# SyncE fetches some rows of the second layer one by one, in place of two GpSimd gathers in one pair of chunks in 20

## The chip, the cores and the metric

The kernel runs on one core of a Trainium2 chip. A core has TensorE (PE in the profile; its weight loads are PEld), VectorE (DVE), ScalarE (ACT), GpSimd (POOL) and SyncE (SP). SyncE does no arithmetic on tensors; it issues transfers and can work with registers. The metric is the device time of one execution in microseconds, and the median of several runs is quoted.

## The reference

A graph network with two layers over 12,500 nodes and 200,000 edges. The edges are sorted by their destination.

```python
h = relu(layernorm(x))
x = x + gcn(h)            # out-degree norm, sum over the edges, in-degree norm, 32x32 matrix
h = relu(layernorm(x))
x = x + edge_mlp(h)       # this is the second layer

def edge_mlp(x):          # for each edge from j to i
    msg = concat(x[i], x[j] - x[i])
    h = relu(msg @ W1 + b1)      # 64 to 64
    h = relu(h @ W2 + b2)        # 64 to 128
    h = relu(h @ W3 + b3)        # 128 to 64
    m = h @ W4 + b4              # 64 to 32
    return segment_sum(m, i) / max(count(i), 1)
```

The first product is linear in x[i] and x[j], so it is taken once per node: the kernel keeps two tables in DRAM, `tab_i` and `tab_j`, each with one row of 64 floats per node, and the first hidden layer of an edge is relu(tab_i[i] + tab_j[j]).

## The kernel before

The edges stand in tiles of 128; four tiles make a chunk (512 edges), and two chunks make a pair. There are 391 chunks and so 196 pairs (`NPAIR`). The first layer ends with `update_nodes`, which writes `tab_j` and `tab_i` (L513, L514). The second layer is one loop over pairs, written as a software pipeline with its order fixed by hand:

```python
for m in range(NPAIR + last):
    if m < NPAIR:
        gather_in(m)
    if m + AHEAD + 1 < NPAIR:
        prepare(m + AHEAD + 1)
    advance(running)
    for lag, stage in ((last, fourth), (4, third), (3, second), (1, first)):
```

- `gather_in(m)` lets GpSimd gather the rows of `tab_j` for the eight tiles of pair m, one indirect transfer per tile (L211). Each takes 128 row numbers from `src_j` and brings 128 rows of 256 bytes into the tile `gj`. There are six `gj` buffers.
- `prepare(m)` lets SyncE load what a pair needs besides: `ai`, the window of `tab_i` rows that its sorted destinations fall into (L858, five buffers), and `row`, the destinations relative to that window, repeated on 128 partitions (L861, four buffers). `AHEAD` is 2, so in step m of the loop SyncE issues these for pair m + 3.
- `turn(m)` compares `row` with the partition's number on VectorE (L868), which gives a one-hot matrix `turned`.
- `first(m)` is TensorE's first stage: a small matmul on `gj` (L884), four transposes of `gj` (L888), and the product of `ai` with `turned` added to them (L892). ScalarE applies the relu. `second`, `third` and `fourth` follow three, four and five steps of the loop later: the two further layers (L906, L916), with their evictions on ScalarE (L908) and VectorE (L919), and the sum over destinations (L934).

SyncE executes its instructions in the order of the program: a pair's `ai` and `row` stand behind whatever was issued on SyncE ahead of them. The framework gives SyncE's and ScalarE's transfers eight completion semaphores in turn, so a transfer waits for the one that used its semaphore before.

At L970 every engine loads one number from a tile into a register, and SyncE checks its range there. It is the only register load of the kernel.

Of the kernel before, what the change touches and what calls it, by code (L numbers as in the profile page):

```python
# [8 lines left out]
F32 = mybir.dt.float32  # L9
BF16 = mybir.dt.bfloat16  # L10
F16 = mybir.dt.float16
I32 = mybir.dt.int32
# [4 lines left out]
P = 128  # L17
N_NODES = 12500
N_EDGES = 200000
D = 32  # L20
HID = 64
# [4 lines left out]
OFF = 48  # L26
# [7 lines left out]
TPC = 4  # L34
CHUNK = TPC * P
NCH = -(-N_EDGES // CHUNK)
NTR = -(-N_EDGES // P)
# [39 lines left out]
DPAD = (DIR + NDG * GD) * CHUNK  # L77

PC = 32

NROW = NPAD + P

# [2 lines left out]
def gnn_kernel(  # L85
# [20 lines left out]
    nc = tc.nc  # L106
# [14 lines left out]
    tab_j = dram.tile([NPAD, HID], F32, name="tab_j")  # L121
# [9 lines left out]
    def parts(rows):  # L131

        return rows.rearrange("(p j) c -> p j c", p=NPART)
# [23 lines left out]
    xp = fp.tile([NPART, P, D], F32, name="xp")  # L157
    pieces = [slice(j, j + PC) for j in range(0, P, PC)]
    for at in pieces:
# [5 lines left out]
    o = dst.offset + DIR * CHUNK  # L165
# [3 lines left out]
    ident = const.tile([P, P], F32, name="ident")  # L169
# [40 lines left out]
    def gather(tile_ap, table, col):  # L210
        nc.gpsimd.indirect_dma_start(  # L211
            out=tile_ap, out_offset=None, in_=table,
            in_offset=bass.IndirectOffsetOnAxis(ap=col, axis=0))
# [10 lines left out]
    o = 1 + D  # L224
# [15 lines left out]
    for at in pieces:  # L240
        h, a = hx[:, at, :D], xp[:, at, :]
        m = fp.tile([NPART, PC], F32, name="la_m", bufs=2)
        nc.vector.tensor_reduce(m, a, AX.X, OP.add)
        nc.vector.tensor_scalar(m, m, 1.0 / D, None, op0=OP.mult)
        nc.vector.tensor_sub(h, a, m[:, :, None].to_broadcast([NPART, PC, D]))
        nc.vector.tensor_mul(a, h, h)
        v = fp.tile([NPART, PC], F32, name="la_v", bufs=2)
        nc.vector.tensor_reduce(v, a, AX.X, OP.add)
        nc.vector.tensor_scalar(v, v, 1.0 / D, EPS, op0=OP.mult, op1=OP.add)
        sd = fp.tile([NPART, PC], F32, name="la_sd", bufs=2)  # L250
        nc.scalar.activation(sd, v, AF.Sqrt)
        nc.vector.reciprocal(v, sd)
        nc.vector.scalar_tensor_tensor(
            h, h, 0.0, v[:, :, None].to_broadcast([NPART, PC, D]), op0=OP.max, op1=OP.mult)
        nc.sync.dma_start(parts(tab_h[OFF:, :])[:, at, :], hx[:, at, :])
    first.close()
    src_j = stay.tile([P, NT], I32, name="src_j")

    def gather_chunk(rows, table, g):
        for t in range(min(TPC, NTR - g * TPC)):  # L260
            c = g * TPC + t
            gather(rows[:, t, :], table, src_j[:, c : c + 1])
# [23 lines left out]
    with tc.tile_pool(name="deg", bufs=3) as hp, tc.tile_pool(  # L286
        name="deg_ps", bufs=1, space=bass.MemoryType.PSUM
# [42 lines left out]
        for b in batches:  # L330
            to = min(EARLY, RAW + -(-(EARLY - RAW) * (b // (HG * HT) + AHEAD_HG) // len(batches)))
            if to > gathered:
                c = slice(gathered * TPC, to * TPC)
# [6 lines left out]
            for t in range(b, min(NTR, b + HG * HT)):  # L340
                g, i = divmod(t - b, HT)
# [12 lines left out]
        for at in pieces:  # L354
# [4 lines left out]
            for k in range(3):  # L359
                t = terms[:, :, k * D : (k + 1) * D]  # L360
# [19 lines left out]
        for b in range(0, NT, P):  # L380
            n = min(P, NT - b)
# [51 lines left out]
    with tc.tile_pool(name="flag", bufs=1) as fp, tc.tile_pool(  # L433
        name="flag_ps", bufs=1, space=bass.MemoryType.PSUM
# [131 lines left out]
    def advance(running):  # L566

        for r in list(running):
            if next(r, running) is running:
                running.remove(r)  # L570
# [12 lines left out]
    def halves(m):  # L583
        return [k for k in range(2) if 2 * m + k < NCH]
# [4 lines left out]
    with tc.tile_pool(name="e0", bufs=8) as sp, tc.tile_pool(name="nu", bufs=1) as np_, tc.tile_pool(  # L589
        name="direct", bufs=1) as dp, tc.tile_pool(name="e0_ps", bufs=1, space=bass.MemoryType.PSUM) as pp, tc.tile_pool(  # L590
        name="nu_ps", bufs=1, space=bass.MemoryType.PSUM) as np_ps:
# [194 lines left out]
        for m in range(EARLY, DIR + LAG + 1):  # L786
# [6 lines left out]
            i = m - EARLY  # L793
# [11 lines left out]
            later, r = divmod(i, LATER)  # L805
# [13 lines left out]
    with tc.manual_schedule(), tc.tile_pool(name="prep", bufs=3) as prep, tc.tile_pool(name="e1", bufs=3) as ep, tc.tile_pool(name="fn", bufs=2) as fp, tc.tile_pool(  # L819
        name="p1_ps", bufs=2, space=bass.MemoryType.PSUM  # L820
# [32 lines left out]
        def prepare(m):  # L853

            v = live[m] = {"turned": []}
            n, g = len(halves(m)), 2 * m
            ai = v["ai"] = prep.tile([P, 2, HID], F32, name="ai", bufs=5)
            nc.sync.dma_start(ai[:, :n], bass.AP(  # L858
                tensor=tab_i.tensor, offset=tab_i.offset + STEP * g * HID, ap=[[HID, P], [STEP * HID, n], [1, HID]]))
            row = v["row"] = prep.tile([P, 2, CHUNK], F16, name="row", bufs=4)  # L860
            nc.sync.dma_start(row[:, :n], bass.AP(  # L861
                tensor=rel_row.tensor, offset=rel_row.offset + g * CHUNK, ap=[[0, P], [CHUNK, n], [1, CHUNK]]))

        def turn(m):
            v = live[m]
            for k in halves(m):
                turned = prep.tile([P, CHUNK], F32, name=f"turned{k}", bufs=3)
                nc.vector.tensor_tensor(  # L868
                    turned, v["row"][:, k], part_f.to_broadcast([P, CHUNK]), op=OP.is_equal)
                v["turned"].append(turned)  # L870

        def gather_in(m):
            gj = live[m]["gj"] = ep.tile([P, TPC, 2, HID], F32, name="gj", bufs=6)
            if len(halves(m)) < 2 or (2 * m + 2) * TPC > NTR:
                nc.vector.memset(gj, 0.0)
            for k in halves(m):
                g = 2 * m + k
                gather_chunk(gj[:, :, k, :], tab_j[:, :], g)

        def first(m):  # L880
            v = live[m]
            p1 = pp1.tile([P, TPC, P], F32, name="p1")

            nc.tensor.matmul(  # L884
                p1[:1, 0, : 2 * TPC], ident[:, :1], v["gj"][:, :, :, 0].rearrange("p t k -> p (t k)"), start=True, stop=True,
                skip_group_check=True)
            for t in range(TPC):
                nc.tensor.matmul(  # L888
                    p1[:, t, :], v["gj"][:, t].rearrange("p k c -> p (k c)"), ident, is_transpose=True,
                    start=(t == 0), stop=False, skip_group_check=True)  # L890
            for k in halves(m):
                nc.tensor.matmul(  # L892
                    p1[k * HID : (k + 1) * HID].rearrange("p t e -> p (t e)"), v["ai"][:, k], v["turned"][k],
                    start=False, stop=True, skip_group_check=True)
            h1 = ep.tile([P, CHUNK], F32, name="h1", bufs=4)
            nc.scalar.activation(h1, p1.rearrange("p t e -> p (t e)"), AF.Relu)  # L896
            v["h1"] = h1
# [40 lines left out]
        def add_messages(k4):  # L938
            q, i = divmod(k4, J)
            ps = group_ps.pop(k4)  # L940
            for k in range(2):
                chunks = len(range(k4 * GRP + k, min(NCH, (k4 + 1) * GRP), 2))
                if chunks:
                    s = slice(k * HID, (k + 1) * HID)
                    sums.add(s, P * k4 + STEP * k, ps[s, : 2 * STEP * (chunks - 1) + W])
            if i == J - 1 or k4 == NGRP - 1:
                running.append(finish_nodes(q))
# [4 lines left out]
        last = 5  # L952
        for m in range(NPAIR + last):
            if m < NPAIR:
                gather_in(m)
            if m + AHEAD + 1 < NPAIR:
                prepare(m + AHEAD + 1)
            advance(running)
            for lag, stage in ((last, fourth), (4, third), (3, second), (1, first)):
                if 0 <= m - lag < NPAIR:  # L960
                    stage(m - lag)
                if stage is fourth and m >= lag and ((m - lag) % (GRP // 2) == GRP // 2 - 1 or m - lag == NPAIR - 1):
                    add_messages((m - lag) // (GRP // 2))
            if m + 1 < NPAIR:
                turn(m + 1)
# [5 lines left out]
    with tc.If(bad > 0):  # L971
        sums0 = dram.tile([NROW, D + 1], F32, name="sums0")
        sums1 = dram.tile([NROW, D], F32, name="sums1")
        with tc.tile_pool(name="gp", bufs=1) as gp, tc.tile_pool(name="ge", bufs=1) as ge, tc.tile_pool(
            name="ge_ps", bufs=1, space=bass.MemoryType.PSUM
# [49 lines left out]
            with tc.For_i(0, NTR, 1) as i:  # L1025
                s, d, same, r = edges(i)
# [13 lines left out]
            for q in range(NQ):  # L1040
                n = min(J, NBLK - J * q)
# [10 lines left out]
            with tc.For_i(0, NTR, 1) as i:  # L1052
                s, d, same, r = edges(i)
                gi = ge.tile([P, HID], F32, name="g_gi")
                gather(gi, tab_i[:, :], d)
                gj = ge.tile([P, HID], F32, name="g_gj")
# [27 lines left out]
            c = gp.tile([P, NBLK], F32, name="g_c")  # L1084
# [39 lines left out]
```

## Time and profile before

| | us |
|---|---|
| median of 3 runs | 3516.55 (3509.39 to 3517.01) |
| profiled execution, its own time | 3509.95 |
| its span in the profile | 3508.2 |
| first gather of the second layer | 1525.7 |
| last gather of the second layer ends | 3480.0 |

The span is what the profile covers; the execution's own time is 1.75 us more. The second layer takes from 1525.7 us to the end, some 1980 us for 196 pairs. In the profile's lists a group of instructions is a line of the kernel, an engine, an operation and the tiles by name; then come the count, the busy time with the mean of one in ns, and the idle time of that engine just before these instructions with what ended most of it. "issue" means that nothing which the profile shows was waited for. Instructions that only SyncE's sequencer handles (SPq) are not counted as busy, but appear in the answers for a line and in the waits.

### The profile page before, as it was taken

Reading aid. Unit: us, or ns where it says so; the run is one execution under the profiler, and the core shown is the slowest. Engines: PE = TensorE matmul, PEld = TensorE weight load, DVE = VectorE, ACT = ScalarE, POOL = GpSimd, SP = SyncE. Lnnn points to the kernel's source line nnn. Section 1 sums busy time; section 2 is a strip of 40 time slices with the busy share of each in tenths; the row PEclk is TensorE's granted clock in tenths of the full one; section 3 lists DMA queues with packets and bytes.
Section 4 is the critical chain, followed back from the end, with each engine's and each line's share of the span. In section 5 each row is a group of like instructions: output and inputs, shape, how many; then the busy total and the mean of one; then the engine's idle time right before and its main releaser. Section 6 shows DMA issues by size and latency. Waiting matters only on the chain. (4 is left out here: it accounts for less than half of the span.)

```text
span 3508.2 us, 54111 instructions
## 1 busy us (share of the span) xinstructions
PE 2569.0 (73%) x20860; PEld 1819.5 (52%) x20860; DVE 1807.6 (52%) x4040; ACT 1140.6 (33%) x2092; POOL 2504.7 (71%) x2655
## 2 busy tenths in 40 slices
PE   3772888787787778748767777777777777777777
PEld 2661666566665666625445454444444444454454
DVE  7995877677776777523333333333333333333333
ACT  0003666566675666411222112121221212222111
POOL 7777777666665666647777777777777777777775
PEclk9755999889898998857887878888887787878778
DMA  4113112111121111212222222222222222222221
GB/s 94 15 15 78 27 27 33 29 31 30 24 37 24 29 30 26 48 45 61 62 58 61 61 61 60 59 62 61 61 60 60 61 62 58 61 61 61 59 60 31
DMA packets 234631, 170.64 MB, mean 49 GB/s; under 512 B 156008, under 2 KB 182856, under 8 KB 234368
## 3 DMA queue, kind: packets, MB, share of 16 engines
q0 software_dynamic: 84320, 75.96, 13.6%
q1 hardware_dynamic: 131306, 85.26, 8.9%
q10 hardware_dynamic: 18742, 5.89, 0.9%
q8 instruction: 168, 2.75, 0.3%
q14 instruction: 95, 0.78, 0.1%
HBM read 153.98 MB, written 12.92 MB: 48 GB/s over the span
## 5 line engine op out<-in xcount | busy, mean ns | idle before, releaser
L211 POOL DMA_INDIRECT gj<-tab_j,src_j x1563 | 1478.0, 946 | 512.0 <-issue 423.8
L211 POOL DMA_INDIRECT rows<-tab_hn,src_j x816 | 771.9, 946 | 380.2 <-issue 203.5
L919 DVE TENSOR_TENSOR h<-p,b3n 128x512 f32<-128x512 f32 x196 | 135.3, 690 | 746.3 <-PE p L916 746.3
L775 ACT ACTIVATE count<-count_two 128x858 bf16<-128x858 f32 x491 | 434.5, 885 | 261.2 <-PE count_two L773 230.1
L723 PE MATMUL st<-count,table 128*128 128x104 bf16 (+1 forms) x6076 | 393.4, 223 | 67.2 <-ACT count L775 64.6
L916 PE MATMUL p<-w3s,h 128*128 128x64 f32 x3128 | 441.3, 300 | 0.2 <-ACT h L908 0.2
L916 PEld LDWEIGHTS p<-w3s,h 128*128 128x128 f32 x3128 | 413.5, 213 | 47.6 <-issue 39.4
L908 ACT ACTIVATE h<-p,b2s 128x1024 f32<-128x1024 f32 x196 | 218.0, 1112 | 658.5 <-PE p L906 658.5
L723 PEld LDWEIGHTS <-table 128*128 128x128 bf16 x6076 | 367.4, 103 | 116.4 <-issue 48.3
L884 PE MATMUL p<-gj,ident 128*1 128x8 f32 x392 | 39.1, 174 | 513.6 <-DMA gj<-tab_j,src_j 513.6
L773 PE MATMUL count_two<-oh,lo 128*128 128x429 bf16 x982 | 294.7, 384 | 128.3 <-ACT count L775 118.2
L884 PEld LDWEIGHTS p<-gj,ident 128*1 128x1 f32 x392 | 21.8, 80 | 684.7 <-issue 672.0
L896 ACT ACTIVATE h<-p 128x512 f32<-128x512 f32 x196 | 117.1, 597 | 797.3 <-PE p L892 797.3
L712 DVE TENSOR_TENSOR oh<-keys,kept 128x2574 bf16<-128x2574 f16 x246 | 364.9, 1487 | 3.6 <-PE count_third L773 3.6
L934 PEld LDWEIGHTS ps<-hot,h 128*64 128x64 f32 x3126 | 270.7, 189 | 176.4 <-issue 165.1
L892 PE MATMUL p<-turned,ai 128*64 128x512 f32 x782 | 330.4, 937 | 0.0
L552 DVE TENSOR_TENSOR acc<-acc,ps 64x64 f32<-64x64 f32 (+1 forms) x198 | 44.7, 226 | 522.7 <-PE ps L934 490.0
L934 PE MATMUL ps<-hot,h 128*64 128x128 f32 x3126 | 295.8, 351 | 0.5 <-DVE h L919 0.5
L211 POOL DMA_INDIRECT rows_early<-tab_h,src_j x224 | 215.6, 963 | 71.5 <-issue 49.4
L868 DVE TENSOR_TENSOR turned<-row,kept 128x512 f32<-128x512 f16 x391 | 249.4, 679 | 26.8 <-PE p L892 22.0
L773 PEld LDWEIGHTS <-lo 128*128 128x128 bf16 x1473 | 140.5, 105 | 222.9 <-issue 169.2
L775 ACT ACTIVATE count<-count_third 128x416 bf16<-128x416 f32 x491 | 251.6, 512 | 0.0
(201 smaller groups left out, 3182.8 us busy)
## 6 DMA issues: line engine op xcount, KB each, us to landing
row<-rel_row SPq DMA_DIRECT2D x195, 256.0 KB
gj<-tab_j,src_j POOLq DMA_INDIRECT x1563
rows<-tab_hn,src_j POOLq DMA_INDIRECT x816
ai<-tab_i SPq DMA_DIRECT2D x195, 64.0 KB
srow<-hi_row SPq DMA_DIRECT2D x64, 98.0 KB
rows_early<-tab_h,src_j POOLq DMA_INDIRECT x224
tab_j<-nu_aij SPq DMA_DIRECT2D x24, 128.0 KB
tab_i<-nu_aij SPq DMA_DIRECT2D x24, 128.0 KB
```

The costliest lines, as they stand in the source:

```text
L211: nc.gpsimd.indirect_dma_start(out=tile_ap, out_offset=None, in_=table, in_offset=bass.IndirectOffsetOnAxis(ap=col, axis=0))
L712: nc.vector.tensor_tensor(oh, keys[:, :, i : i + 2][:, :, None, :].to_broadcast([P, 3, KW, 2]), count_h[:, None, :, :].to_broadcast([P, 3, ...
L723: nc.tensor.matmul(ps[:, : tiles * WD], table[:, h, :], c[:, :tiles, h, :], start=(h == 0), stop=(h == PART - 1))
L773: nc.tensor.matmul(ps[:, k, :w], lo[:, i % TPC // 2, :, i % 2], oh[:, k0 + k, :w, i % 2], start=True, stop=True)
L775: nc.scalar.activation(counts[g][:, t, a:b, :].rearrange("p (k h) d -> p k (h d)", k=len(ranges)), ps[:, :, :w], AF.Copy)
L868: nc.vector.tensor_tensor(turned, v["row"][:, k], part_f.to_broadcast([P, CHUNK]), op=OP.is_equal)
L892: nc.tensor.matmul(p1[k * HID : (k + 1) * HID].rearrange("p t e -> p (t e)"), v["ai"][:, k], v["turned"][k], start=False, stop=True, skip_ ...
L896: nc.scalar.activation(h1, p1.rearrange("p t e -> p (t e)"), AF.Relu)
L908: nc.scalar.activation(h2[:, :n], p2[:, :n], AF.Relu, bias=b2s)
L916: nc.tensor.matmul(p3[:, k * TPC + t, :], v["h2"][:, k, t * P : (t + 1) * P], w3s, start=True, stop=True)
L919: nc.vector.tensor_tensor(h3[:, :n], p3[:, :n], b3n[:, None, :].to_broadcast([P, n, HID]), op=OP.max)
L934: nc.tensor.matmul(ps[k * HID : (k + 1) * HID, o : o + W], v["h3"][:, k * TPC + t, :], v["hot"][k][:, t, :], start=(i == 0 and t == 0), st ...
```

## The change

In nine pairs (19, 39, 59 and so on up to 179) the last tile of both chunks is no longer gathered by GpSimd. Its 256 rows are fetched by SyncE into a tile of their own, `gj_last`, row by row. The new function `fetch(m)` stands ahead of `gather_in(m)` in each step of the loop. In steps 0 to 15 of each block of 20 it works for the pair at the end of that block: it loads 16 row numbers from a small tile `one` into SyncE's registers and issues 16 transfers of one row each; in step 0 it also loads `one` with the 256 numbers. `first` then transposes `gj_last` in place of the last tile of `gj`, and its small matmul leaves that tile out.

```diff
+EVERY, FETCH = 20, 16
...
+        fetched = {}
+
+        def fetch(m):
+
+            s = m + EVERY - m % EVERY - 1
+            i = m % EVERY
+            if i >= FETCH or 2 * s + 2 > NCH or (2 * s + 2) * TPC > NTR:
+                return
+            if i == 0:
+                one = prep.tile([1, 2, P], I32, name="one", bufs=2)
+                o = src.offset + 2 * s * CHUNK + (TPC - 1) * P
+                nc.sync.dma_start(one, bass.AP(tensor=src.tensor, offset=o, ap=[[0, 1], [CHUNK, 2], [1, P]]))
+                fetched[s] = ep.tile([P, 2, HID], F32, name="gj_last", bufs=2), one
+            last, one = fetched[s]
+            n = 2 * P // FETCH
+            k, e = divmod(i * n, P)
+            _, values = nc.values_load_multi_w_load_instructions(
+                one[:, k, e : e + n], engines=[mybir.EngineType.SP], min_val=0, max_val=N_NODES)
+            for r, v in enumerate(values):
+                nc.sync.dma_start(last[e + r : e + r + 1, k, :], tab_j[bass.ds(v + OFF, 1), :])
+
         def gather_in(m):
             gj = live[m]["gj"] = ep.tile([P, TPC, 2, HID], F32, name="gj", bufs=6)
+            if m in fetched:
+                for k in halves(m):
+                    for t in range(TPC - 1):
+                        c = (2 * m + k) * TPC + t
+                        gather(gj[:, t, k, :], tab_j[:, :], src_j[:, c : c + 1])
+                return
...
         def first(m):
...
+            last, _ = fetched.pop(m, (None, None))
+            n = TPC if last is None else TPC - 1
...
-                p1[:1, 0, : 2 * TPC], ident[:, :1], v["gj"][:, :, :, 0].rearrange("p t k -> p (t k)"), start=True, stop=True,
+                p1[:1, 0, : 2 * n], ident[:, :1], v["gj"][:, :n, :, 0].rearrange("p t k -> p (t k)"), start=True, stop=True,
...
-                    p1[:, t, :], v["gj"][:, t].rearrange("p k c -> p (k c)"), ident, is_transpose=True,
+                    p1[:, t, :], (v["gj"][:, t] if t < n else last).rearrange("p k c -> p (k c)"), ident, is_transpose=True,
...
             if m < NPAIR:
+                fetch(m)
                 gather_in(m)
```

`values_load_multi_w_load_instructions` becomes one register load of 16 numbers and, for each number, a fused register operation and an assertion that check it against the limits. Each row's address is worked out by one more fused register operation (plus `OFF`, times the row's size) ahead of its transfer.

## The prediction

> **What bounds the kernel now.** I start with the busy times on the page, then the costliest groups, because the change touches only the second layer, and there one group stands out.
>
> ```profile
> PE 2569.0 (73%) x20860; PEld 1819.5 (52%) x20860; DVE 1807.6 (52%) x4040; ACT 1140.6 (33%) x2092; POOL 2504.7 (71%) x2655
> ...
> L211 POOL DMA_INDIRECT gj<-tab_j,src_j x1563 | 1478.0, 946 | 512.0 <-issue 423.8
> ...
> L884 PE MATMUL p<-gj,ident 128*1 128x8 f32 x392 | 39.1, 174 | 513.6 <-DMA gj<-tab_j,src_j 513.6
> ```
>
> TensorE looks as busy as GpSimd over the whole span, but that mixes stages. The second line is GpSimd's work in the second layer: 1563 gathers of 946 ns, with idle time of the kind "issue", which is no wait for anybody. The third line says that TensorE stands idle in the same layer for 513.6 us, and waits for exactly these gathers. So GpSimd sets the pace. The timeline in the middle of the layer gives that pace:
>
> ```profile
> 2503.58 0.95 POOL L211 DMA_INDIRECT gj<-tab_j,src_j  x1 [0.30 <-issue]
> ...
> 2504.83 0.95 POOL L211 DMA_INDIRECT gj<-tab_j,src_j  x1 [0.30 <-issue]
> ...
> 2509.26 0.36 SPq L858 DMA_DIRECT2D ai<-tab_i  x1
> ...
> 2509.71 0.42 SPq L861 DMA_DIRECT2D row<-rel_row  x1
> ```
>
> A gather starts every 1.25 us, eight make a pair of chunks: 10.0 us per pair. The last two lines are all that SyncE does in that pair. What it does otherwise is in its own waits (total us, times, longest):
>
> ```profile
> SPq L858 <- PE p L892: 1718.2, 191, 17.3
> ```
>
> 1718.2/191 = 9.0 us per pair: SyncE stands before the ai load of a pair three ahead, whose buffer (five of them) an earlier pair still holds. That idle time is what the change wants to spend. Is it enough?
>
> **The Trainium skill.** "DMA: Bandwidth & Descriptors", section "Issuing engines are not separate DMA queues", says that issuing from several engines saves only the sequencer's time to initiate a transfer. This fits here: the page shows the 16 DMA engines at 2 tenths in the second layer, while GpSimd's issue sets the pace. "Perfetto Trace Analysis", section "Per-instruction lifecycle: what the profiler-reported window actually captures", says that the shown duration of a SyncE transfer is the sequencer's part and excludes the data movement; here the row load shows 0.42 us for 256 KB, so these durations are SyncE's own cost, and I add them up as such.
>
> **The change, on GpSimd.** Nine pairs (19, 39 up to 179) lose two of eight gathers: 18 gathers, and the built program has 1545 instead of 1563. 18 x 1.25 us = 22.5 us, all on the path, if nothing else becomes late. TensorE can take this: in the tail of the timeline, where gathers no longer hold it, one pair's first matmul (L884) follows another's by 7.2 us (3477.87 to 3485.08), less than the 7.5 us of six gathers. The edits in first() (one short matmul over 6 columns instead of 8, transposes that read another tile) change nothing in number or size that matters: under 0.01 us in nine pairs.
>
> **The change, on SyncE.** In 16 of each 20 pairs, from pair 0 to pair 175 (9 x 16 = 144 times), SyncE now issues ahead of ai and row: one load of 16 registers, 16 range checks (a fused register operation and an assertion each), and 16 times a fused register operation (add, multiply, multiply) and a transfer of one row of 256 bytes. That is 2304 transfers. The trace of before shows one of each kind; columns are duration ns minimum, median, maximum, and starts:
>
> ```profile
> L970 SPq TENSOR_LOAD <-bad_i x1: 468/468/468, 312.6 to 312.6; - x1
> L970 SPq FUSED_REGOPS  x1: 177/177/177, 313.2 to 313.2; - x1
> L970 SPq SEQ_ASSERT  x1: 32/32/32, 313.4 to 313.4; - x1
> ```
>
> ```profile
> L207 ACTq DMA_DIRECT2D w1s<-in_b x1: 291/291/291, 20.9 to 20.9; - x1
> ```
>
> The last is the nearest to a row: 64 floats to one partition, though on ScalarE's queue and with a fixed address. Between two SyncE instructions lies a gap: from the end of ai (2509.62) to the start of row (2509.71) there are 0.09 us with a 17 ns semaphore wait inside, so 0.07 us in two gaps, and 0.04 on ScalarE's queue ahead of L207. I take 0.045 each; the starts of the three L970 lines, 0.2 apart for the assertion after 177 ns, agree.
>
> Per pair with a fetch:
> - register load: 0.468 + 0.045 = 0.51 for one register. Fifteen more are in no trace. "Runtime: NRT & Kernel Launch", section "Instruction fetch mechanics", gives "~200 ns/register even for bulk" for register loads of the runtime; "DMA: Bandwidth & Descriptors", section "Latency and other measured facts", gives about 600 ns as the floor of one load, against 468 here, and says that several are bundled to spread it. So between 0 and 0.2 us each; I take the middle, 0.1: 2.01 us, an estimate.
> - checks: 16 x (0.177 + 0.045 + 0.032 + 0.045) = 4.78 us.
> - rows: 16 x (0.177 + 0.045 + 0.291 + 0.045) = 8.93 us. Both ends for the transfer: 0.29, and the 0.42 of SyncE's row load, which has 128 partitions.
> - ai and row as before, with two semaphore waits of 17 ns: 0.36 + 0.42 + 2 x 0.017 + 4 x 0.045 = 0.99 us.
>
> T = 16.7 us. With free extra registers it is 15.2; with 0.2 us each and 0.42 us per transfer, 16.7 + 1.5 + 2.1 = 20.3.
>
> **What stands behind it.** GpSimd takes 20 pairs in 158 x 1.25 = 197.5 us. SyncE needs 16 T + 4 x 0.99, which is 271 us at 16.7. The limit is T = 12.1. Behind the fetches in SyncE's order stand ai and row; row feeds the comparison on VectorE (L868), that feeds the matmul L892, and everything later in the pair. The loads are issued three pairs ahead, which covers some 25 us once and is used up after four fetches. From then on TensorE waits for row, GpSimd for its six gj buffers, and SyncE is the bound; the 22.5 us on GpSimd are then worth nothing.
>
> **The sum.** The fetches can begin when the second layer does, at 1525.7 us (first gj gather). SyncE then works through pairs 0 to 175: 144 x 16.7 + 32 x 0.99 = 2437 us, to 3962. It has then issued row for pair 178. Eighteen pairs remain, without fetches: 6 us until pair 178 has been through L892 (3 for landing, 3 for comparison and matmuls, estimates from the timeline), about 12 pairs that GpSimd has not yet gathered at 10.0 us, and the drain after the last gather, which before was 3508.2 - 3480.0 = 28.2 us. 3962 + 6 + 120 + 28 = 4116 us of span, against the 3508.2 of the profiled execution. Its own time was 3509.95, 1.75 more, and the median of the runs is 6.6 above that: 4116 + 8 = 4124, rounded to 4125. Each us of T moves this by 144 us.
>
> Other costs: the list of 256 numbers is nine small loads and is used at once by the register load that waits for it, a few us nine times, at most 30 us. Other buffers: gj_last has two, of which the older is free a block before. The 2304 rows are 0.6 MB over DMA engines that are busy for a quarter: nothing. Not costed: a little time in which SyncE, in the four pairs without fetch, still waits for an ai buffer.
>
> **Rivals.**
> - *SyncE keeps pace* (the other side: faster). The 9.0 us of idle hold the fetch, and the eighteen gathers are saved: 3516.55 - 22.5 = 3494. It decides at T below 12.1 us (11.1 for the fetch). For it: three of my prices are single records, and FUSED_REGOPS may be slow the first time. At 0.08 in place of 0.177, T falls by 3.1 to 13.6, still too much; also registers for nothing: 12.1. So two prices must be wrong the same way. Chance 0.10.
> - *Registers and transfers at the high end.* T = 20.3: 4116 + 144 x 3.6 = 4634. Nothing in the profile excludes it, since no transfer with a register address is there.
> - *Completion, not issue.* Eight semaphores go round, so each transfer waits for the one eight before. With 16 rows in 8.93 us this is hidden up to 8 x 0.56 = 4.5 us from issue to completion. At 6 us, the rows take 16 x 6/8 = 12 us, T = 19.8, and the time is 4560. Against it: srow, issued in the same way, was waited for 2.6 us at the longest.
> - *It does not do what it says.* A scheduler might leave the gathers; the built program shows 1545, so this is excluded.
>
> **How the numbers follow.** SyncE as the bound near 16.7: 0.58; the two dearer rivals together 0.18; a T between 12.2 and 13.8 (cheaper register work, still slower): 0.12; SyncE keeps pace: 0.10; both effects cancel within 0.2% (7 us, about what a measurement of this kernel can tell): 0.02. Slower 0.88, same 0.02, faster 0.10. The range runs from T = 13.8 (3700) to 20.4 (4650); below it lie the fast case and part of the cheaper one, some 0.15, above it 0.04.
>
> **What would show it.** Right: the group L211 gj x1545; SyncE's waits on L858 fall from 1718 us to below 100; TensorE and VectorE wait for row where they waited for gj; GpSimd's idle before gj names TensorE; starts of row 16 to 18 us apart in a block. Per step: FUSED_REGOPS 177, SEQ_ASSERT 32, a 16-register load near 2.0 us, a row transfer near 0.29. Wrong: SyncE still waits several us per pair on L858 in the fetch pairs, with gathers 1.25 us apart throughout.

## The result, and the profile after

The changed kernel takes 3687.98 us (median of 6 runs, 3685.38 to 3691.85) against 3511.18 us (median of 6) for the kernel before: a ratio of 1.0502, 95% interval 1.0488 to 1.0516. It is 177 us slower. The profiled execution took 3685.38 us, with a span of 3683.6.

In part of the experiments below the kernel before itself took 4355 to 4402 us; of those runs the ratio to the runs of the kernel before beside them is used, and their own traces.

First a line of the page of before, then the page of the changed kernel, its busy times and two of its groups. (L214 is the old L211, L871 the old L868.)

```profile
L868 DVE TENSOR_TENSOR turned<-row,kept 128x512 f32<-128x512 f16 x391 | 249.4, 679 | 26.8 <-PE p L892 22.0
```

```profile
PE 2653.1 (72%) x20860; PEld 1882.4 (51%) x20860; DVE 1808.0 (49%) x4040; ACT 1135.1 (31%) x2092; POOL 2488.9 (68%) x2637
...
L214 POOL DMA_INDIRECT gj<-tab_j,src_j x1545 | 1461.1, 946 | 705.4 <-issue 421.3
...
L871 DVE TENSOR_TENSOR turned<-row,kept 128x512 f32<-128x512 f16 x391 | 250.5, 682 | 1113.1 <-DMA row<-rel_row 1086.7
```

The 18 gathers are gone: 1545, and GpSimd's busy time on them fell from 1478.0 to 1461.1 us. But its idle time before them grew from 512.0 to 705.4, so it no longer sets the pace: 193.4 us more idle and 16.9 us less busy are 176.5 us, the whole loss. The group that now waits is VectorE's comparison: 1086.7 us for `row`. Before, its idle time there was 26.8 us, most of it for TensorE. The waits of all engines in the changed kernel show who passes this on:

```profile
DVE turned L871 <- DMA row<-rel_row: 1086.7, 129, 11.4
...
PE kept L848 <- DVE turned L871: 275.3, 23, 20.1
...
PE ps L966 <- DVE h L951: 271.1, 75, 9.5
...
POOL gj L214 <- PE p L920: 210.4, 38, 18.7
```

Read downward: `row` is late, and VectorE waits for it 129 times. TensorE waits for VectorE's comparison (L871), and also for its eviction L951, which stands behind the comparisons in VectorE's order. So TensorE's transposes (L920) come late, and GpSimd waits for a `gj` buffer. Is `row` late because its transfer is slow, or because it was issued late? One pair in the timeline:

```profile
2549.23 0.42 SPq L864 DMA_DIRECT2D row<-rel_row  x1
...
2552.93 1.28 DVE L871 TENSOR_TENSOR turned<-row,kept 128x512 f32<-128x512 f16 x2 [10.29 <-DMA row<-rel_row]
```

VectorE had stood for 10.3 us, but the transfer had been issued only 3.7 us earlier. In the packets that the traces keep, the last of the 128 packets of a `row` ends 3.17 us after its issue (median), against 3.14 us before. The transfer is as fast as it was. But where the kernel before issued `row` 24.7 us ahead of its comparison (median), the comparisons that wait here start 3.6 us after the issue. `row` is issued late. SyncE's own waits show why:

```profile
SPq L861 <- PE p L924: 94.2, 27, 11.3
...
SPq L891 <- DMA one<-in_src: 15.2, 7, 3.2
```

SyncE's wait for TensorE ahead of the `ai` load (L861, before L858) was 1718.2 us and is 94.2. SyncE is busy with instructions, and `row` stands behind them. The timeline of SyncE in one fetch pair shows the period:

```profile
2535.83 0.42 SPq L864 DMA_DIRECT2D row<-rel_row  x1
2541.72 6.92 SPq L894 DMA_DIRECT2D gj_last<-tab_j  x16
2548.74 0.40 SPq L861 DMA_DIRECT2D ai<-tab_i  x1
2549.23 0.42 SPq L864 DMA_DIRECT2D row<-rel_row  x1
```

From one `row` to the next 13.4 us go by. 5.5 us of them lie between the end of `row` and the first row transfer (the register load and the checks), 6.9 us are the sixteen transfers with their address work, and the rest is `ai` and `row`. The median step from one `ai` to the next, over the 161 steps above 5 us, is 13.36 us; GpSimd would need 10.0.

The answers for the two lines of the fetch give the price of each instruction (minimum, median and maximum in ns, then first and last start):

```profile
L891 SPq FUSED_REGOPS  x2304: 147/147/169, 1480.2 to 3518.4; - x192
L891 SPq SEQ_ASSERT  x2304: 18/18/31, 1480.4 to 3518.6; - x192
L891 SPq TENSOR_LOAD <-one x144: 1137/1166/1487, 1478.6 to 3513.0; - x144
```

```profile
L894 SPq FUSED_REGOPS  x2304: 46/46/51, 1521.7 to 3525.0; - x192
L894 SPq MOVE gj_last<-tab_j x2304: 29/29/39, 1523.4 to 3525.1; - x192
L894 SPq DMA_DIRECT2D gj_last<-tab_j x2304: 224/227/322, 1523.5 to 3525.2; - x192
```

The gaps between them are mostly 43 ns in the trace, 31 ns ahead of a row's transfer and 54 ns behind a register load.

### The profile page after: what moved, and what is told of

Its sections match the earlier page's. It is cut to its first block, busy times and chain, and to the rows that moved or that the text cites. A ratio compares the mean times of both kernels' runs of the same rounds, so it can differ in the third digit from the quotient of the medians.

```text
span 3683.6 us, 65806 instructions
## 1 busy us (share of the span) xinstructions
PE 2653.1 (72%) x20860; PEld 1882.4 (51%) x20860; DVE 1808.0 (49%) x4040; ACT 1135.1 (31%) x2092; POOL 2488.9 (68%) x2637
## 5 line engine op out<-in xcount | busy, mean ns | idle before, releaser
L214 POOL DMA_INDIRECT gj<-tab_j,src_j x1545 | 1461.1, 946 | 705.4 <-issue 421.3
L214 POOL DMA_INDIRECT rows<-tab_hn,src_j x816 | 772.4, 947 | 377.0 <-issue 204.4
L871 DVE TENSOR_TENSOR turned<-row,kept 128x512 f32<-128x512 f16 x391 | 250.5, 682 | 1113.1 <-DMA row<-rel_row 1086.7
L948 PE MATMUL p<-w3s,h 128*128 128x64 f32 x3128 | 534.4, 342 | 0.3 <-ACT h L940 0.3
L948 PEld LDWEIGHTS p<-w3s,h 128*128 128x128 f32 x3128 | 503.2, 252 | 48.2 <-issue 36.0
L966 PE MATMUL ps<-hot,h 128*64 128x128 f32 x3126 | 281.2, 338 | 271.1 <-DVE h L951 271.1
L966 PEld LDWEIGHTS ps<-hot,h 128*64 128x64 f32 x3126 | 237.1, 174 | 430.3 <-ACT acc L553 194.2
L938 PE MATMUL p<-h,w2s 64*128 64x512 f32 x782 | 303.0, 860 | 0.0
L553 ACT ACTIVATE acc<-ps 64x128 f32<-64x128 f32 (+2 forms) x230 | 52.8, 248 | 733.6 <-DVE acc L555 733.6
L951 DVE TENSOR_TENSOR h<-p,b3n 128x512 f32<-128x512 f32 x196 | 134.9, 688 | 281.9 <-PE p L948 280.3
L924 PE MATMUL p<-turned,ai 128*64 128x512 f32 x782 | 266.3, 765 | 0.0
L214 POOL DMA_INDIRECT rows_early<-tab_h,src_j x224 | 216.2, 965 | 72.3 <-issue 50.0
L578 DVE TENSOR_TENSOR hot<-rel_h,kept 128x512 f32<-128x512 f16 x391 | 249.1, 678 | 0.0
L848 PE MATMUL kept<-w4s,acc 128*128 128x32 f32 x198 | 41.2, 365 | 275.7 <-DVE turned L871 275.3
```

What stands on the lines that cost most here:

```text
L214: nc.gpsimd.indirect_dma_start(out=tile_ap, out_offset=None, in_=table, in_offset=bass.IndirectOffsetOnAxis(ap=col, axis=0))
L578: nc.vector.tensor_tensor(hot, rel_h[:, g * TPC : (g + 1) * TPC][:, :, None].to_broadcast([P, TPC, W]), lanes_f[:, None, :W].to_broadcast( ...
L871: nc.vector.tensor_tensor(turned, v["row"][:, k], part_f.to_broadcast([P, CHUNK]), op=OP.is_equal)
L924: nc.tensor.matmul(p1[k * HID : (k + 1) * HID].rearrange("p t e -> p (t e)"), v["ai"][:, k], v["turned"][k], start=False, stop=True, skip_ ...
L938: nc.tensor.matmul(p2[:, k], w2s[s, :], v["h1"][s, :], start=True, stop=True)
L948: nc.tensor.matmul(p3[:, k * TPC + t, :], v["h2"][:, k, t * P : (t + 1) * P], w3s, start=True, stop=True)
```

## The experiments

The theory was that SyncE's instruction time per fetch pair, and nothing else, makes `row` late. The rivals: the 2304 small transfers disturb gathers and loads in the DMA engines; the lead of three pairs is too short for the bursts; the saved gathers count for nothing anyhow.

**No range checks (m_no_checks).**

```diff
             _, values = nc.values_load_multi_w_load_instructions(
-                one[:, k, e : e + n], engines=[mybir.EngineType.SP], min_val=0, max_val=N_NODES)
+                one[:, k, e : e + n], engines=[mybir.EngineType.SP], min_val=0, max_val=N_NODES,
+                skip_runtime_bounds_check_because="row numbers of the graph")
```

> The changed kernel without the range checks of the 16 row numbers. SyncE's work per fetch pair falls from 13.35 to about 9.3 us where instructions take what they took in the changed kernel's profile, below the 10.0 us that GpSimd takes for a pair: 3487 us where the kernel before takes 3509, ratio 0.9936. If the 2304 small transfers disturb the gathers or the row loads in the DMA engines, the time stays above that of before. Where the kernel before takes about 4391 us, 1.025 again.

Measured: 3488.04 us against 3507.82, ratio 0.9939 (0.9925 to 0.9952), 1 us from the expectation. Its page and SyncE's waits:

```profile
L214 POOL DMA_INDIRECT gj<-tab_j,src_j x1545 | 1457.8, 944 | 506.5 <-issue 418.6
...
L871 DVE TENSOR_TENSOR turned<-row,kept 128x512 f32<-128x512 f16 x391 | 249.9, 681 | 26.3 <-PE p L925 21.5
```

```profile
SPq L861 <- PE p L925: 486.2, 105, 11.5
```

SyncE has idle time again, `row` is no longer named as a cause of VectorE's idle time, and GpSimd's idle time is what it was before (506.5 us against 512.0). All 2304 transfers are still issued here, and all read and write what they did. So the transfers alone did not make the loss. Without the 4.0 us of checks in each of 144 pairs it is gone, and the saved gathers come through: 3507.82 - 3488.04 = 19.8 us (17 to 26 by the interval), with 22.5 worked out. This version beats both kernels, the one before by 0.6%.

The changed kernel itself ran beside it as a reference (m_after):

> The changed kernel unaltered, as the reference for the runs with the gathers kept, the longer lead and no checks where the kernel before takes about 4391 us (those gave ratios of 1.156 to 1.159, 1.146 to 1.156 and 1.023 to 1.030). If SyncE is the bound, this is within 0.01 of the first two: 1.15 to 1.16 there. If the gathers count, the changed kernel is 22 us or more below the one that keeps them: 1.150 or less. Where the kernel before takes 3509 us it is 1.050 as measured before.

3688.35 us, ratio 1.0512 (1.0496 to 1.0528), the result once more. These runs also speak against one more rival, the clock that TensorE is granted, as a share of full speed. It was 0.77 in the profiled execution of the changed kernel and 0.82 in that of before, but two runs here with 0.76 and 0.80 took 3688.38 and 3688.33 us.

**The checks kept, but half the rows per pair (g_spread).**

```diff
-EVERY, FETCH = 20, 16
+EVERY, FETCH = 32, 32
```

> The changed kernel with EVERY, FETCH = 32, 32: the checks stay, 8 rows per pair instead of 16, one fetched pair in 32. SyncE's work per pair where a transfer and a check take what they took in the changed kernel's profile: one load of 8 registers 0.8, checks 8 x 0.252 = 2.0, rows 8 x 0.417 = 3.3, ai and row 1.0, in sum 7.2 us, in every pair and below 10.0. Six pairs are fetched (31 to 191), 12 gathers saved, 15 us: 3496 us where the kernel before takes 3511, ratio 0.9957. If checks as such or transfers as such were the harm, and not their sum per pair, two thirds of the 177 us loss should remain: about 3610 us.

Measured: 3498.41 us against 3508.28, ratio 0.9967 (0.9956 to 0.9978): 9.9 us saved (7.7 to 15.4 by the interval), of 15 worked out. Checks and rows of the same kind as in the changed kernel, 1536 of each, no longer make `row` late once a pair holds only eight of each. SyncE's waits and the page:

```profile
SPq L861 <- PE p L924: 455.1, 166, 8.9
```

```profile
L214 POOL DMA_INDIRECT gj<-tab_j,src_j x1551 | 1463.5, 944 | 507.9 <-issue 426.2
```

Together the two runs settle the cause: it is the sum of SyncE's instruction time. The transfers stay in the first run and the checks in the second, so neither makes the loss alone. Taking away instructions and spreading them out both bring SyncE's work in a fetch pair under GpSimd's 10.0 us (to 9.3 and 7.2 us, as worked out in the expectations), and both turn the loss into a gain. Whether the pair or the block of 20 pairs is the period that counts isn't separated: in both runs SyncE's work lies below GpSimd's on either count.

**Where the kernel before took 4355 to 4402 us.** The first four runs fell there. No checks (e1_no_checks):

> The changed kernel without the range checks of the 16 row numbers (16 fused register operations of 147 ns and 16 assertions of 18 ns per fetch pair, with 43 ns gaps: 16 x 0.252 = 4.0 us). SyncE's work per fetch pair falls from 13.35 to about 9.3 us, below the 10.0 us that GpSimd takes for a pair. If SyncE's instruction time is the whole cause, the loss goes and the 18 saved gathers come through: 3511 - 22.5 = 3489 us, ratio to before 0.9936, gathers 1.25 us apart throughout, SyncE waiting for L924 again. If instead the 2304 small transfers disturb the gathers or the row loads in the DMA engines, they still do so here and the time stays above 3511 us. If the saved gathers bring nothing for another reason, it is 3511 us.

Ratio 1.0299 (1.0280 to 1.0319). Half the rows per pair (e2_spread):

> The changed kernel with EVERY, FETCH = 32, 32: the checks stay, 8 rows per pair instead of 16, one fetched pair in 32. SyncE's work per pair: one load of 8 registers 0.8, checks 8 x 0.252 = 2.0, rows 8 x 0.417 = 3.3, ai and row 1.0, in sum 7.2 us, in every pair and below 10.0. Six pairs are fetched (31 to 191), 12 gathers saved, 15 us: 3496 us, ratio 0.9957. If checks as such or the transfers as such were the harm, and not their sum per pair, two thirds of the 177 us loss should remain: about 3610 us.

Ratio 1.0125 (1.0104 to 1.0146). All gathers kept (e3_keep_gathers):

> The changed kernel, but GpSimd gathers all eight tiles of the nine pairs as before too; SyncE's fetches stay and are used. Theory that SyncE is the bound: the 18 gathers lie beside SyncE's work, the time stays at 3688 us within 5 us. Rival, that the gathers still count: 3688 + 22 = 3710 us.

Ratio 1.1576 (1.1550 to 1.1601). Longer lead (e4_lead):

> The changed kernel with ai and row loaded six pairs ahead instead of three, eight and seven buffers instead of five and four. If SyncE's work over 20 pairs is the bound (16 x 13.35 + 4 + 4 = 222 us against 197.5), more lead buys only once what it covers (three pairs, about 30 us) and the short waits for ai buffers (some 30 us in all): 3630 to 3670 us. If the loss came from too little lead in bursts, it goes: about 3490 us.

Ratio 1.1542 (1.1514 to 1.1569).

The times in microseconds that these expect are for a kernel before at 3511 us. The ratios that they expect, 0.9936 without checks and 0.9957 with half the rows, were missed. Four more runs of the version without checks missed theirs in the same way:

> The changed kernel without the range checks of the 16 row numbers, once more, since on the chip of the first try the kernel before itself took 4395 us[...]. Checks per fetch pair: 16 x (147 + 43 + 18 + 43 ns) = 4.0 us. SyncE's work per fetch pair falls from 13.35 to about 9.3 us, below the 10.0 us that GpSimd takes for a pair. If SyncE's instruction time is the whole cause, the loss goes and the 18 saved gathers come through: 3511 - 22.5 = 3489 us, ratio 0.9936, and SyncE waits for L925 again. If the 2304 small transfers disturb the gathers or the row loads in the DMA engines, they still do so here and the time stays above 3511 us. If the saved gathers bring nothing for another reason, it is 3511 us.

> The changed kernel without the range checks of the 16 row numbers. Checks per fetch pair: 16 x (147 + 43 + 18 + 43 ns) = 4.0 us. SyncE's work per fetch pair falls from 13.35 to about 9.3 us, below the 10.0 us that GpSimd takes for a pair. If SyncE's instruction time is the whole cause, the loss goes and the 18 saved gathers come through: about 22.5 us below the kernel before, 3487 where that takes 3509, ratio 0.9936. If the 2304 small transfers disturb the gathers or the row loads in the DMA engines, they still do so here and the time stays above that of before. If the saved gathers bring nothing for another reason, it is equal to before.

> The changed kernel without the range checks of the 16 row numbers. Checks per fetch pair: 16 x (147 + 43 + 18 + 43 ns) = 4.0 us. SyncE's work per fetch pair falls from 13.35 to about 9.3 us, below the 10.0 us that GpSimd takes for a pair. If SyncE's instruction time is the whole cause, the loss goes and the 18 saved gathers come through: about 22.5 us below the kernel before, 3487 where that takes 3509, ratio 0.9936. If the 2304 small transfers disturb the gathers or the row loads in the DMA engines, they still do so here and the time stays above that of before. If the saved gathers bring nothing for another reason, it is equal to before.

> The changed kernel without the range checks of the 16 row numbers. Checks per fetch pair: 16 x (147 + 43 + 18 + 43 ns) = 4.0 us. SyncE's work per fetch pair falls from 13.35 to about 9.3 us, below the 10.0 us that GpSimd takes for a pair. If SyncE's instruction time is the whole cause, the loss goes and the 18 saved gathers come through: about 22.5 us below the kernel before, 3487 where that takes 3509, ratio 0.9936. If the 2304 small transfers disturb the gathers or the row loads in the DMA engines, they still do so here and the time stays above that of before. If the saved gathers bring nothing for another reason, it is equal to before.

Ratios 1.0275, 1.0274, 1.0263 and 1.0225. A time above that of before is what the rival with the small transfers expects, so the traces have to tell the two apart. The step of SyncE from `ai` to `ai` had a median of 14.6 us (e1_no_checks) and 12.0 us (e2_spread) there, instead of 9.7 and 9.8. Single instructions of SyncE stood there: in the second layer of e1_no_checks 882 of its register operations and transfers took over 0.5 us, most of them some 0.7, and 617 us in all; in the same kernel's run above (m_no_checks) 18 did, with 15 us. So without checks SyncE was late again, and VectorE waited 308.3 us for `row`. With half the rows it did not (its idle time there was 41.5 us, 32.5 of them for TensorE), and what made that run 1.25% slower is not shown. Nor is it shown what slowed the kernel before, since it has no trace from there.

Three variants ran only there. The first keeps all gathers and fetches besides (e3_keep_gathers above, and g_keep_gathers):

```diff
         def gather_in(m):
...
-            if m in fetched:
+            if False:
```

> The changed kernel, but GpSimd gathers all eight tiles of the nine pairs as before too; SyncE's fetches stay and are used. Theory that SyncE is the bound: the 18 gathers lie beside SyncE's work, the time stays at 3688 us within 5 us. Rival, that the gathers still count: 3688 + 22 = 3710 us.

Ratio 1.1587 (1.1560 to 1.1614). A further run gave 1.1564:

> The changed kernel, but GpSimd gathers all eight tiles of the nine pairs as before too; SyncE's fetches stay and are used. Theory that SyncE is the bound: the 18 gathers lie beside SyncE's work, the time stays at 3688 us within 5 us. Rival, that the gathers still count: 3688 + 22 = 3710 us.

The second variant loads `ai` and `row` six pairs ahead (e4_lead above, and g_lead):

```diff
+LEAD = 6
...
-            ai = v["ai"] = prep.tile([P, 2, HID], F32, name="ai", bufs=5)
+            ai = v["ai"] = prep.tile([P, 2, HID], F32, name="ai", bufs=8)
...
-            row = v["row"] = prep.tile([P, 2, CHUNK], F16, name="row", bufs=4)
+            row = v["row"] = prep.tile([P, 2, CHUNK], F16, name="row", bufs=7)
...
-            if m + AHEAD + 1 < NPAIR:
-                prepare(m + AHEAD + 1)
+            if m + LEAD < NPAIR:
+                prepare(m + LEAD)
```

> The changed kernel with ai and row loaded six pairs ahead instead of three, eight and seven buffers instead of five and four. If SyncE's work over 20 pairs is the bound (16 x 13.35 + 4 + 4 = 222 us against 197.5), more lead buys only once what it covers (three pairs, about 30 us) and the short waits for ai buffers (some 30 us in all): 3630 to 3670 us. If the loss came from too little lead in bursts, it goes: about 3490 us.

Ratio 1.1564 (1.1537 to 1.1591). A further run gave 1.1464, where 1.035 to 1.046 was expected:

> The changed kernel with ai and row loaded six pairs ahead instead of three, eight and seven buffers instead of five and four. If SyncE's work over 20 pairs is the bound (16 x 13.35 + 4 + 4 = 222 us against 197.5), more lead buys only once what it covers (three pairs, about 30 us) and the short waits for ai buffers (some 30 us in all): 3630 to 3670 us where the kernel before takes 3509, ratio 1.035 to 1.046. If the loss came from too little lead in bursts, it goes: about 3490 us.

The waits of all engines with the longer lead:

```profile
DVE turned L872 <- DMA row<-rel_row: 1289.6, 108, 18.9
POOL gj L215 <- PE p L921: 901.4, 90, 27.6
```

Six pairs of lead do not cure it: VectorE still waits 1289.6 us for `row`. That fits a limit of rate, which lead can only put off; a short lead in bursts, whose loss should have gone, is out for the SyncE step of that run, 17.8 us. At 13.4 us a longer lead was not run. But SyncE's own waits in the changed kernel leave it little: of the 2002 us from the first row transfer to the last (1523.5 to 3525.2) some 50 us are waits and about 1950 are work, where GpSimd would need about 1740 us for its 1392 gathers of the same 176 pairs, at 1.25 us each. How much either variant differs from the changed kernel is not settled, since the changed kernel has no run beside the same before time. In particular, that the 18 gathers count for nothing while SyncE is late was argued, and not shown.

The third has no checks and a fetched pair in every 16 (n_no_checks_16):

```diff
-EVERY, FETCH = 20, 16
+EVERY, FETCH = 16, 16
```

> No range checks, and EVERY, FETCH = 16, 16: one fetched pair in 16, so twelve pairs and 24 gathers saved, 30 us. SyncE's work is then 9.3 us in every pair plus 4 us per block for the list of numbers, 152.8 us per 16 pairs, against GpSimd's 126 x 1.25 = 157.5. If the sum over a block decides, SyncE just keeps pace: about 3479 us where before takes 3509, ratio 0.9915. If the row loads become late at 97% of SyncE's time, it falls behind the variant with EVERY = 20 and no checks: above 3488 us.

Ratio 1.0774 (1.0744 to 1.0804), after two runs with 1.0786 and 1.0690:

> No range checks, and EVERY, FETCH = 16, 16: one fetched pair in 16, so twelve pairs and 24 gathers saved, 30 us. SyncE's work is then 9.3 us in every pair plus 4 us per block for the list of numbers, 152.8 us per 16 pairs, against GpSimd's 126 x 1.25 = 157.5. SyncE just keeps pace: about 3479 us where before takes 3509, ratio 0.9915. If the row loads become late at 97% of SyncE's time, it falls behind the variant with EVERY = 20: above 3487 us.

> No range checks, and EVERY, FETCH = 16, 16: one fetched pair in 16, so twelve pairs and 24 gathers saved, 30 us. SyncE's work is then 9.3 us in every pair plus 4 us per block for the list of numbers, 152.8 us per 16 pairs, against GpSimd's 126 x 1.25 = 157.5. SyncE just keeps pace: about 3479 us where before takes 3509, ratio 0.9915. If the row loads become late at 97% of SyncE's time, it falls behind the variant with EVERY = 20: above 3487 us.

With SyncE's step at a median of 14.2 us there, far above what the expectation rests on, this says nothing on a SyncE at 97%. Whether this version would beat 3488 us, and the exact point from which SyncE decides, stay open.

## Why the prediction was right and where it was wrong

It said 4125 us, range 3700 to 4650, and slower with 0.88. Slower was right; 3688 lies below the range.

**Right: what bounds, and how it is passed on.** SyncE is the bound, at 13.36 us per fetch pair against a limit of 12.1; `row` is late, and VectorE, TensorE and GpSimd follow. The signs of this path came: gj x1545; SyncE's wait on L861 (the old L858) below 100 us (94.2, though just); VectorE waiting for `row`; TensorE as the longest cause of GpSimd's idle time but for "issue". The signs of size did not: the step between `row` loads is 13.4 us and not 16 to 18, and the four prices per instruction all came lower.

**Wrong: T, the work per fetch pair.** Forecast 16.7 us, measured 13.36. Term by term, with durations from the two line answers and the gaps of the trace:

| term | forecast us | measured us |
|---|---|---|
| register load of 16 | 2.01 | 1.166 + 0.054 = 1.22 |
| 16 checks | 4.78 | 16 x (0.147 + 0.018 + 2 x 0.043) = 4.02 |
| 16 rows | 8.93 | 16 x (0.046 + 0.029 + 0.227 + 0.117 of gaps) = 6.70 |
| `ai` and `row` | 0.99 | about 1.0 |
| pauses of 0.35 us, see the end; slower first transfers | none | about 0.35 |

The largest error is in the rows: 2.2 of 3.3 us. The step that failed is to price the address work by the one fused register operation in the trace of before, 177 ns. That one checks a number against limits; the one that works out an address took 46 ns, 2.1 us less for 16. An additional MOVE of 29 ns, not foreseen, took part of that back. A row's transfer took 227 ns, under the 291 taken as its lower end, 1.0 us less for 16. The checks were 147 and 18 ns instead of 177 and 32. The extra registers, where the Trainium skill's page "Runtime: NRT & Kernel Launch", section "Instruction fetch mechanics", has about 200 ns each for its own kind of load, took (1166 - 468)/15 = 47 ns each here: of the bounds 0 and 0.2, the middle was twice too much.

**The sum otherwise held.** 3.34 us less per fetch pair over 144 pairs take 481 us off, 4116 - 481 = 3635 us of span. The measured 3683.6 is 49 more, and it brought the time nearer to the forecast, not the working. Two things that the prediction left out of its sum fill that. The end of a block in the timeline of SyncE shows the one:

```profile
2633.09 0.38 SPq L861 DMA_DIRECT2D ai<-tab_i  x1
2634.90 0.33 SPq L864 DMA_DIRECT2D row<-rel_row  x1
2635.32 0.66 SPq L886 DMA_DIRECT2D one<-in_src  x1
2650.71 0.40 SPq L861 DMA_DIRECT2D ai<-tab_i  x1
```

From `ai` to `ai` 17.6 us instead of 13.4: the list of numbers is issued, SyncE waits for it at once, and `row` waited 1.4 us besides. That is about 4 us at four of the eight block ends. At the other four SyncE waits some 6 us for an `ai` buffer, as named but not costed, and the list then costs 2 to 3 us more. Together this makes some 50 us: about 25 for the list, which the prediction bounded by 30 and then didn't add, and about 25 for the buffers. The tail after the last fetch was forecast at 154 us and took 3683.6 - 3525.2 = 158.

**Why the range missed.** The working moved T to 15.2 and 20.3 by the two prices that no trace showed. The single records of before (468, 177, 32 and 291 ns) stood at face value even at the lower end, while the text itself said that a single record may be slow the first time. The range then reached down to T = 13.8, and the 13.36 that came lies in the stretch from 12.2 to 13.8, which had a chance of 0.12. In the rival "SyncE keeps pace", 0.08 us for FUSED_REGOPS was tried: with it T was 13.6. That is close to what came, in part by luck, since the other prices in it were still too high and the MOVE and the pauses were missing. A lower end built from that, some 3680 us, would have held 3688, if narrowly.

The rival "completion, not issue" fell: the semaphore wait inside the sixteen transfers hardly appears, 6.6 to 6.9 us for 16 rows being nearly all issue and gaps. "Registers and transfers at the high end" fell with the prices above.

## What to carry to other kernels

An idle engine has a budget per period, and work handed to it has to fit into that period with everything that stands behind it in its queue: 9.0 us were free, 12.4 were added, and 177 us came of 22 saved. Count every register operation and check beside the transfers, since the checks of 16 numbers cost SyncE more than half of what the transfers and their addresses did. Without the checks, or with half as many rows per pair, the same idea gains 20 and 10 us; when a price comes from a single record of a similar instruction, let the range follow that price down as well as up.

## What the runs showed of the hardware

Instructions of one name can differ threefold: the fused register operation that checks a number against its limits took 147 ns, the one that works out an address 46 ns. What makes the difference was not tested. On SyncE one load of 1 register took 468 ns (a single record, in the trace of before), of 8 registers 718 (in g_spread) and of 16 registers 1166.

In the changed kernel's trace SyncE pauses for some 0.35 us at 100 places in the second layer, 93 of them exactly 128 instructions after the last, 35 us in all. A queue of kind "instruction" on the page rose by 92 packets of 8192 bytes (q14: 95 to 187 packets), one for every 127 of the 11,695 instructions that the trace has more. The run without checks agrees: it has 4608 fewer instructions on SyncE and 36 fewer packets in this queue (151), which is one for every 128, and its pauses fall to some 70. "Runtime: NRT & Kernel Launch", section "Instruction fetch mechanics", says of instruction fetch that a block boundary is "mostly hidden", and speaks of 16 KiB blocks; on SyncE in this kernel the packets are of 8 KiB, and there are about as many pauses as further packets. That these pauses are the fetch is read from the equal spacing and the equal numbers; no run varied the fetch itself.
